# A graph layer with gathered keys and values on one core: the instructions of the last three quads in another order, the last quad cut in three tiles and one, and two normalizations on GpSimd

## The chip, the cores and the metric

The kernel runs on one core of one Trainium2 chip. The metric is device time in microseconds (us), the median of the runs shown; less is better. Beside the runs there is one profiled execution of the kernel, with a trace of its instructions and transfers. Engines are named as in the profile: PE is TensorE's matmul, PEld its weight load, DVE VectorE, ACT ScalarE, POOL GpSimd, SP SyncE, which here only issues transfers. A "q" behind a name (SPq, POOLq) is that engine's sequencer, which issues, waits and branches.

## What is computed

`x` has 6250 nodes of 128 features; there are 206250 edges, sorted by the node `dst` that receives; an edge takes k and v at `src` and q at `dst`, and adds into `dst`.

```python
w = silu(edge_attr_32 @ rad_W1 + rad_b1) @ rad_W2 + rad_b2
w = w + silu(edge_attr_32_n2 @ sph_W1 + sph_b1) @ sph_W2 + sph_b2   # edges x 8 heads x 16
q, k, v = x @ Wq, x @ Wk, x @ Wv                                    # nodes x 8 heads x 16
alpha = (q[dst] * w * k[src]).sum(-1) / sqrt(16) * edge_weight      # edges x 8
out = segment_sum(alpha[..., None] * v[src], dst) / 16
y = x + out
return (y - mean(y)) / sqrt(var(y) + 1e-5)                          # per node
```

## The kernel before

**Tiles.** A tile is 128 edges, a quad 4 tiles (512 edges), a group 4 quads (2048 edges). There are 101 groups (`NG`) and 403 quads; the last group, number 100, has three quads. Within a group the quads are worked on in the order 0, 2, 1, 3 (`order`), so the last three quads of the program are called `a`, `b`, `c` = `order[-3:]`. In SBUF a quad's edges lie on the 128 partitions, 4 tiles of 128 columns each.

**A quad's work.** PE makes the two hidden layers (`first_layers`, L552, tile `ph`), ACT applies silu (`silus`, L584), PE makes q at the edges with a one-hot matrix (`q_at_edges`, L561, tile `pq`) and the second layers with the bias (`weigh`, L599 and L604, tile `pw`). GpSimd gathers k and v of the senders from a table in DRAM (`gathers`, L140, tile `kv`, four transfers a quad, in a ring of 16 buffers that have a semaphore each; `kv_done` holds the semaphore and the count that a quad's reader waits for). DVE then runs, in this order: `multiply` (L618: q times k), `scores` (L626: times w, L628: sum over each head, L632: times the edge's weight) and `messages` (L645: alpha times v). PE sums the messages of a group into four windows of 32 nodes (`sum_quads`, L657, tile `po`), ACT copies them out (`part_sums`, L693), PE places them into the group's 128 nodes and adds what the group before left over (`sum_group`, L698 and L700; its one-hot matrices are made on DVE by `place`, L687 and L688, tile `to`), and ACT copies the total (L702, tile `tot`).

**Rows.** In 60 of the 403 quads the fourth tile's rows are loaded one by one from SP's and ACT's queues (L211, tile `wide`) instead of by GpSimd; quad `b` is one of them, `c` is not.

**Normalization.** `moments` adds x (L715, tile `y`), and takes mean and variance on DVE (L717 `st`, L718 `mv`). For most groups the inverse root is made on DVE (`inverse_roots`), for the last four it is a square root on ACT (`roots`, L723, `sd`) and a reciprocal on DVE (L741, `rs`); ACT then writes the normalized rows (`scaled`, L736) with a `shift` made on DVE (L730), and SP stores them (`write_rows`, L774). Windows of neighbouring groups overlap in `out`, so each store waits until the store before it has landed.

**Order.** Nothing is scheduled by a planner: the program is recorded as written (`tc.manual_schedule`), each engine executes its instructions in that order, and waits are put in from the tiles that are read and written. One iteration of the main loop (from L810) weighs quad i+1, applies silu for i+2, gathers for i+14, multiplies i+1 and makes the messages of i. The loop ends with group 99 (`NG - 2`); what follows, from L881 on, is written out by hand for group 100. There `sum_wide` (L679) adds `a`, `b` and `c` straight into the 128 nodes with wide one-hots (`wide_one_hots`, L665 to L668, tile `hots`, made on DVE in groups 98 and 99; `weigh_wide` puts the edge weights into them on ACT, so that `scores(..., weighted=False)` needs no L632).

**PSUM.** There are two banks each for `ph`, `pq` and `pw`, one for `po` and one that holds `side`. Before, the end uses a `pq` bank for the totals of groups 98 and 99 and a `ph` bank for the sum of group 100.

**After the last store** every engine reaches the branch at L1035 (a general path, not taken with this data) and the closing instructions at L1087.

## Time and profile before

| what | value |
|---|---|
| device time, median of 3 runs | 2671.97 us |
| the three runs | 2673.54, 2659.76, 2671.97 us |
| the profiled execution: its device time | 2669.98 us |
| the profiled execution: its span in the trace | 2668.2 us |
| mean granted TensorE clock in it | 0.814 |
| instructions | 57891 |
| busy: PE, PEld, DVE, ACT, POOL | 2191.4, 1790.8, 1526.5, 651.5, 1472.9 us |

How to read it: the span runs from the first to the last instruction in the trace; the device time has 1.8 us more around it. Rows of the timeline have the start in us, the length in us, the engine, the line, the operation and its operands (result first), and in brackets for how long the engine had been idle and what ended it. Rows of the windows have the stretch, its length, the busy time of PE, PEld, DVE, ACT and POOL with the number of instructions, the granted TensorE clock, the share of the DMA engines' time and GB/s. Rows by line have the engine's sequencer, operation, count, shortest, median and longest duration in ns, and the first and the last start.

### The profile page before, as it was taken

How to read it: one execution, taken by the hardware profiler on the slowest of the kernel's cores; microseconds unless marked ns; L12 is line 12 of the kernel's file. 1: busy time of each engine (PE TensorE's matmuls, PEld its weight loads, DVE VectorE, ACT ScalarE, POOL GpSimd, SP SyncE). 2: the span in 40 equal slices, each digit the busy share in tenths (PEclk: the TensorE clock that was granted, in tenths of full speed). 3: DMA queues.
4: the chain of work that ended last, by engine and by line, in shares of the span. 5: the costliest groups of instructions: out<-in, count | busy, mean ns of one | idle time of the engine just before them, and what ended most of it. 6: DMA issues, size and time to landing. Idle time of an engine off the chain costs nothing.

```text
span 2668.2 us, 57891 instructions
## 1 busy us (share of the span) xinstructions
PE 2191.4 (82%) x15990; PEld 1790.8 (67%) x15990; DVE 1526.5 (57%) x3424; ACT 651.5 (24%) x1360; POOL 1472.9 (55%) x1562
## 2 busy tenths in 40 slices
PE   5688888788888888888887888888788888888888
PEld 3466666676766676666666676676666766667676
DVE  2456555656555555655555655555555555556557
ACT  1122222222222222222222222222222222222223
POOL 4365555555556555555555555555555555555550
PEclk7788878878878887887888878877788787777889
DMA  5433343443334343343434434333333433334331
GB/s 178 137 117 111 114 117 112 118 117 111 116 107 119 109 121 115 112 120 108 121 110 119 119 108 118 112 117 110 115 119 112 116 110 118 116 114 115 116 104 35
DMA packets 154089, 305.48 MB, mean 114 GB/s; under 512 B 40748, under 2 KB 88220, under 8 KB 153756
## 3 DMA queue, kind: packets, MB, share of 16 engines
q0 software_dynamic: 73984, 201.43, 26.8%
q1 hardware_dynamic: 70352, 95.81, 11.0%
q10 hardware_dynamic: 9420, 4.47, 0.7%
q8 instruction: 127, 2.08, 0.3%
q14 instruction: 206, 1.69, 0.2%
HBM read 288.10 MB, written 13.46 MB: 113 GB/s over the span
## 4 chain that ended last, share of the span: by engine, by line
PE 67%; issue 16%; SPq 7%; DVE 6%; another core or an unknown queue 3%; ACTq 0%; DMA 0%; ACT 0%; DVEq 0%
PE pw L604 33%; PE ph L552 10%; PE pq L561 10%; PE po L657 6%; SPq L211 5%; PE pw L599 3%; PE pq L283 2%; PE pq L698 1%; DVE kq L618 1%; PE pk L378 1%; SPq L205 1%; PE pq L700 1%; DVE side L628 1%; PE pq L274 1%
## 5 line engine op out<-in xcount | busy, mean ns | idle before, releaser
L140 POOL DMA_INDIRECT kv<-kv_tab,src_i x1520 | 1440.5, 948 | 1112.2 <-PE pw L604 493.0
L604 PE MATMUL pw<-w,act 128*128 128x128 f32 x6448 | 1091.6, 334 | 70.3 <-issue 69.4
L604 PEld LDWEIGHTS pw<-w,act 128*128 128x128 f32 x6448 | 988.5, 240 | 195.4 <-issue 178.6
L584 ACT ACTIVATE act<-ph,b 128x512 f32<-128x512 f32 x806 | 554.4, 688 | 1899.3 <-PE pw L604 1284.5
L552 PE MATMUL ph<-feats,w 32*128 32x512 f32 x1612 | 677.0, 772 | 149.5 <-issue 141.2
L618 DVE TENSOR_TENSOR kq<-pq,kv 128x512 f32<-128x512 f32 (+1 forms) x403 | 270.7, 672 | 859.6 <-PE pw L604 599.1
L561 PE MATMUL pq<-q,hotT 32*128 32x128 f32 x3224 | 572.9, 328 | 7.1 <-issue 3.6
L561 PEld LDWEIGHTS pq<-q,hotT 32*128 32x128 f32 x3224 | 483.9, 226 | 12.9 <-issue 12.2
L552 PEld LDWEIGHTS ph<-feats,w 32*128 32x128 f32 x1612 | 193.2, 215 | 309.5 <-issue 279.3
L628 DVE TENSOR_REDUCE side<-kq 128x32 f32<-128x512 f32 x403 | 280.1, 695 | 92.2 <-remote 27.4
L645 DVE TENSOR_TENSOR msg<-kv,side 128x512 f32<-128x512 f32 (+1 forms) x404 | 269.4, 667 | 42.8 <-DVE side L632 0.9
L626 DVE TENSOR_TENSOR kq<-pw,kq 128x512 f32<-128x512 f32 x403 | 274.4, 681 | 0.0
L657 PE MATMUL po<-msg,hot 128*32 128x128 f32 x3200 | 191.7, 312 | 33.0 <-issue 32.8
L599 PE MATMUL pw<-brow,onesb 3*128 3x512 bf16 x403 | 182.0, 452 | 0.0
L657 PEld LDWEIGHTS po<-msg,hot 128*32 128x32 f32 x3200 | 84.8, 117 | 90.3 <-issue 63.9
L283 PE MATMUL pq<-wq,xT 128*128 128x128 f32 x200 | 54.7, 362 | 83.6 <-issue 68.0
L698 PE MATMUL pq<-part,to 128*128 128x128 f32 x200 | 53.4, 356 | 68.4 <-issue 34.2
L283 PEld LDWEIGHTS pq<-wq,xT 128*128 128x128 f32 x200 | 35.2, 220 | 109.0 <-issue 88.0
L632 DVE TENSOR_TENSOR side<-side,scale 128x32 f32<-128x32 f32 x400 | 80.0, 200 | 44.9 <-remote 1.7
L698 PEld LDWEIGHTS pq<-part,to 128*128 128x128 f32 x200 | 37.3, 232 | 80.2 <-issue 43.3
L378 PE MATMUL pk<-wkv,xT 128*128 128x256 f32 x162 | 48.5, 442 | 48.3 <-DVE kv L379 39.6
L378 PEld LDWEIGHTS pk<-wkv,xT 128*128 128x128 f32 x162 | 33.3, 221 | 56.9 <-DVE kv L379 38.1
(121 smaller groups left out, 912.9 us busy)
## 6 DMA issues: line engine op xcount, KB each, us to landing
wide<-kv_tab ACTq DMA_DIRECT2D x3960, 1.0 KB
wide<-kv_tab SPq DMA_DIRECT2D x3720, 1.0 KB
feats<-in_edges SPq DMA_DIRECT2D x101, 512.0 KB
kv<-kv_tab,src_i POOLq DMA_INDIRECT x1520
relb<-rel_lin SPq DMA_DIRECT2D x101, 128.0 KB
x<-in_x SPq DMA_DIRECT2D x101, 64.0 KB
out<-y SPq DMA_DIRECT2D x101, 64.0 KB
kv_tab<-kv SPq DMA_DIRECT2D x12, 512.0 KB
```

Of the source, the lines that this page charges most:

```text
L140: return nc.gpsimd.indirect_dma_start(out=o, out_offset=None, in_=table, in_offset=bass.IndirectOffsetOnAxis(ap=index, axis=0))
L283: nc.tensor.matmul(pt[:n, :D], xT_of[g][:, :n], wq, start=True, stop=True)
L552: return nc.tensor.matmul(act_of[q, i], w1[r0:r0 + R, :], feats_of[g][r0:r0 + R, c0:c0 + EQ], start=True, stop=True)
L561: o = nc.tensor.matmul(pq_of[q][:, t, :], hotT_of[g][b, t * P:(t + 1) * P], q_of[g][b, :], start=True, stop=True)
L584: o = nc.scalar.activation(act, act_of[q, i], AF.Silu, bias=b1[:, i:i + 1])
L599: nc.tensor.matmul(pw, onesb, brow.rearrange("p t d -> p (t d)"), start=True, stop=False)
L604: o = nc.tensor.matmul(pw[:, t, :], act_of[q, i][:, t * P:(t + 1) * P], w2[:, i, :], start=False, stop=(t == QT - 1 and i == 1))
L618: o = nc.vector.tensor_tensor(kq_of[q][:, u, :], pq_of[q][:, u, :], kv[:, :, :D], op=OP.mult)
L626: nc.vector.tensor_tensor(m, pw_of[q][:, t, :], m, op=OP.mult)
L628: o = nc.vector.tensor_reduce(alpha, m.rearrange("p t (h e) -> p t h e", e=HD), AX.X, OP.add)
L645: o = nc.vector.tensor_tensor(msg_of[q][:, u, :].rearrange("p t (h e) -> p t h e", e=HD), kv[:, :, D:].rearrange("p t (h e) -> p t h e", e ...
L657: o = nc.tensor.matmul(po_of[g][j * W:(j + 1) * W, :], hot_of[g][:, j * QT + t, :], msg_of[g * NQ + j][:, t, :], start=(t == 0), stop=(t = ...
```

## The change

It does these things, all within groups 97 to 100:

- The fourth tile of the last quad `c` is gathered under a 17th semaphore, and its reader waits for it by itself.
- `multiply`, `scores` and `messages` of `c` are called for tiles 0 to 2 and then for tile 3 instead of for the quad (`messages` had been called for two halves).
- q of `c` is made before the total of group 98; the totals of 98 and 99 use `ph` banks, the sum of group 100 uses the `po` bank. The second layers of `c` come before the total of 99.
- GpSimd adds x for group 98 and 99, as before, and now normalizes them too (subtract the mean, multiply by the inverse root, in one instruction each). ACT's `scaled` and DVE's `shift` for these two are gone; each has a square root and a reciprocal of its own.
- `place` of 98 is made two slots earlier in group 99; `place` of 99 and of 100 and the wide one-hots of `c` are made in group 97 instead of 99.

```diff
-    kv_sems = [tc.alloc_semaphore(f"kv_{n}") for n in range(RING)]
+    kv_sems = [tc.alloc_semaphore(f"kv_{n}") for n in range(RING + 1)]
@@ gathers
+            last = (q, t) == (order[-1], QT - 1)
+            n = RING if last else at
...
-            tc.add_to_no_dep_group(f"kv_{q}", o.ins)
+            tc.add_to_no_dep_group("kv_last" if last else f"kv_{q}", o.ins)
@@ multiply
+            if q == order[-1] and t.stop == QT:
+                waits.append(("kv_last", (kv_sems[RING], kv_count[RING])))
@@
+        def added(g):
+            nc.gpsimd.tensor_tensor(y0(g), tot_of[g], x_of[g], op=OP.add)
@@ main loop
-                if slot == 2 and 1 <= g:
+                if slot == (2 if g < NG - 2 else 0) and 1 <= g:
                     place(g - 1)
...
+                if g == NG - 4 and slot == 0:
+                    place(NG - 2)
+                if g == NG - 4 and slot == 1:
+                    wide_one_hots(order[-1])
+                if g == NG - 4 and slot == 3:
+                    place(NG - 1)
...
                 if g == NG - 2 and slot == 0:
-                    wide_one_hots(order[-1])
                     n = nc.values_load(general, min_val=0, max_val=1)
-                    place(g)
-                    place(NG - 1)
@@ behind the loop
         first_layers(c)
         mark = q_at_edges(b)
-        marks = weigh(b)
-        turned = sum_group(g - 2)
-        for t in range(QT):
-            sum_quads(g - 1, t)
-        silus(c, mark, marks)
+        weigh(b)
+        silus(c, mark)
...
+        def normalized(g, engine, total):
+            i, y = g - (NG - LB), y0(g)
+            engine.tensor_scalar(y, total, y0_of[NG - LB][1][:, i, 0:1], rs[:, i:i + 1],
+                                 op0=OP.subtract, op1=OP.mult)
...
+        roots(g - 3, g - 2)
+        write_rows(len(written))
+        messages(a, scores(a, weighted=False))
+        multiply(b, mark)
+        mark = q_at_edges(c)
+        turned = sum_group(g - 2, "ph")
+        for t in range(QT):
+            sum_quads(g - 1, t)
+        inverses(g - 3, g - 2)
+        shift = shifts(g - 3, g - 2, rs)
+        scaled(g - 3, rs[:, 0:1], shift[:, 0:1], 0)
...
-        mark = q_at_edges(c)
-        turned = sum_group(g - 1)
-        marks = weigh(c)
+        weigh(c)
+        turned = sum_group(g - 1, "ph")
         turned()
-        po_of[g] = pp.tile([P, EQ], F32, name="ph", bufs=2)[:, :D]
+        messages(b, scores(b, weighted=False))
+        po_of[g] = pp.tile([P, D], F32, name="po")
...
-        moments(g - 2, tot_of[g - 2], nc.gpsimd)
-        multiply(c, mark)
-        moments(g - 1, tot_of[g - 1], nc.gpsimd)
-        sd = roots(g - 2, g)
-        normalize(g - 2, g, sd)
-        write_rows(len(written))
-        alpha = scores(c, weighted=False)
-        for h in halves:
-            messages(c, alpha[:, h], h)
-            for t in range(h.start, h.stop):
-                sum_wide(c, t, stop=(t == QT - 1))
-        moments(g, po_of[g], added=True)
+        for i, t in ((g - 2, slice(0, QT - 1)), (g - 1, slice(QT - 1, QT))):
+            added(i)
+            moments(i, None, added=y0(i))
+            roots(i, i + 1)
+            multiply(c, mark if t.start == 0 else None, t)
+            inverses(i, i + 1)
+            normalized(i, nc.gpsimd, y0(i))
+            send(i, nc.sync)
+            messages(c, scores(c, t, weighted=False), t)
+            for i in range(t.start, t.stop):
+                sum_wide(c, i, stop=(i == QT - 1))
+        moments(g, None, added=po_of[g])
...
-        nc.sync.dma_start(out[N - P:, :], y)
+        nc.sync.dma_start(out[N - P:, :], y0(g))
```

**DVE in group 97.** The first place is DVE's order from the one-hots of group 97 (`hot`) to the messages of the loop's second slot. Before:

```order
L294 TENSOR_TENSOR hot<-rel,side 128x512
L618 TENSOR_TENSOR kq<-pq,kv 128x512
L626 TENSOR_TENSOR kq<-pw,kq 128x512
L628 TENSOR_REDUCE side<-kq 128x32
L632 TENSOR_TENSOR side<-side,scale 128x32
L645 TENSOR_TENSOR msg<-kv,side 128x512
L289 TENSOR_TENSOR hotT<-relb,side 128x512
L268 TENSOR_TENSOR pick<-side,off 128x128
L618 TENSOR_TENSOR kq<-pq,kv 128x512
```

The same piece with the change (the lines are numbered anew there: L623 is the old L618, L631 L626, L633 L628, L650 L645):

```order
L692 TENSOR_SCALAR to_42872<-side,rowq 128x128
L693 TENSOR_SCALAR to_42872<-side,rowp 128x128
L623 TENSOR_TENSOR kq<-pq,kv 128x512
L631 TENSOR_TENSOR kq<-pw,kq 128x512
L633 TENSOR_REDUCE side<-kq 128x32
L637 TENSOR_TENSOR side<-side,scale 128x32
L650 TENSOR_TENSOR msg<-kv,side 128x512
L291 TENSOR_TENSOR hotT<-relb,side 128x512
L270 TENSOR_TENSOR pick<-side,off 128x128
L670 CAST d<-dst_i 128x4
L671 TENSOR_SCALAR d<-d,gb 128x4
L673 TENSOR_TENSOR hots<-d,side 128x512
```

Five instructions stand here that stood in group 99, and a sixth (`to` of group 100) follows two slots later.

**DVE at the last quad.** The second place is DVE's order from the mean and variance of group 98 to the end. Before:

```order
L717 BN_STATS st<-y_43818 128x6
L718 BN_AGGR mv<-st 128x2
L618 TENSOR_TENSOR kq<-pq,kv 128x512
L717 BN_STATS st<-y_43818 128x6
L718 BN_AGGR mv<-st 128x2
L741 RECIPROCAL rs<-sd 128x2
L730 SCALAR_TENSOR_TENSOR shift<-mv,rs 128x2
L626 TENSOR_TENSOR kq<-pw,kq 128x512
L628 TENSOR_REDUCE side<-kq 128x32
L645 TENSOR_TENSOR msg<-kv,side 128x256 x2
L717 BN_STATS st<-ph 128x6
```

With the change, from the first `kq` of `c` on:

```order
L623 TENSOR_TENSOR kq<-pq,kv 128x384
L897 RECIPROCAL rs<-sd 128x1
L631 TENSOR_TENSOR kq<-pw,kq 128x384
L633 TENSOR_REDUCE side<-kq 128x24
L650 TENSOR_TENSOR msg<-kv,side 128x384
L728 BN_STATS st<-y_43818 128x6
L729 BN_AGGR mv<-st 128x2
L623 TENSOR_TENSOR kq<-pq,kv 128x128
L897 RECIPROCAL rs<-sd 128x1
L631 TENSOR_TENSOR kq<-pw,kq 128x128
L633 TENSOR_REDUCE side<-kq 128x8
L650 TENSOR_TENSOR msg<-kv,side 128x128
```

The quad's three wide operations are now six, the statistics of group 99 stand between them, and a `shift` is gone.

**GpSimd's end.** The third place is GpSimd's last work before the branch at the end (L1035 before, L1052 with the change). Before:

```order
L140 DMA kv<-kv_tab,src_i 128x256 x1520
L873 TENSOR_LOAD general
L715 TENSOR_TENSOR y_43818<-tot,x 128x128 x2
L1035 COMPARE_AND_BRANCH
L1043 COMPARE_AND_BRANCH
```

With the change:

```order
L140 DMA kv<-kv_tab,src_i 128x256 x1520
L875 TENSOR_LOAD general
L717 TENSOR_TENSOR y_43818<-tot,x 128x128
L901 TENSOR_SCALAR y_43818<-y_43818,mv,rs 128x128
L717 TENSOR_TENSOR y_43818<-tot,x 128x128
L901 TENSOR_SCALAR y_43818<-y_43818,mv,rs 128x128
L1052 COMPARE_AND_BRANCH
L1060 COMPARE_AND_BRANCH
```

Each sum is now followed by its normalization, which reads the reciprocal of its group, and the branch follows the second one.

82 lines of the change are left out of this document (37 added, 45 removed).

## The prediction

> **What bounds the kernel now.** First the chain of waits on the page, by engine: PE holds two thirds of it over the whole span.
>
> ```profile
> PE 67%; issue 16%; SPq 7%; DVE 6%; another core or an unknown queue 3%; ACTq 0%; DMA 0%; ACT 0%; DVEq 0%
> ```
>
> The change begins in group 97, so the view that counts is a table of busy times by stretch, cut where the chain of waits passes from one engine to another (length, then busy us of PE, PEld, DVE, ACT, POOL, then the clock).
>
> ```profile
> 2596.00:2617.30 21.30, 21.04 (x205) 17.60 (x205) 17.56 (x36) 7.21 (x16) 0.00 (x0) 1.00 0.17 52
> 2632.40:2642.30 9.90, 9.21 (x72) 7.73 (x72) 8.62 (x19) 3.35 (x9) 0.00 (x0) 0.66 0.02 4
> 2642.30:2649.84 7.54, 7.54 (x72) 6.47 (x72) 6.84 (x15) 4.25 (x10) 0.00 (x0) 1.00 0.10 27
> 2649.84:2655.20 5.36, 5.30 (x65) 4.47 (x65) 5.19 (x12) 3.79 (x9) 0.65 (x2) 1.00 0.15 43
> 2655.20:2662.20 7.00, 5.05 (x43) 4.67 (x42) 4.97 (x16) 1.47 (x4) 0.27 (x1) 1.00 0.09 23
> 2662.20:2668.20 6.00, 0.00 (x0) 0.00 (x0) 0.00 (x0) 0.00 (x0) 0.00 (x0) 0.63 0.08 19
> ```
>
> In group 97 (first row) PE is full and DVE has 21.30 - 17.56 = 3.74 us to spare. From 2642.3 to 2655.2 both are nearly full, and the chain runs over DVE. At the last quad neither is full: there it is one thing after another. The last 6 us hold no work of a compute engine at all. Before 2596 us nothing is reordered, so 97% of the span can differ only by scatter.
>
> **The work that moves between groups 97 and 99.** Rows of the timeline of DVE:
>
> ```profile
> 2617.34 0.56 DVE L618 TENSOR_TENSOR kq<-pq,kv 128x384 f32<-128x384 f32 x1 [1.33 <-DVEq L615]
> ...
> 2636.04 0.16 DVE L665 CAST d<-dst_i 128x4 f32<-128x4 int32 x1
> ...
> 2637.93 0.68 DVE L618 TENSOR_TENSOR kq<-pq,kv 128x512 f32<-128x512 f32 x1
> ...
> 2642.29 0.69 DVE L618 TENSOR_TENSOR kq<-pq,kv 128x512 f32<-128x512 f32 x1 [0.58 <-PE pq L561]
> ...
> 2645.39 0.34 DVE L687 TENSOR_SCALAR to<-side,rowq 128x128 f32<-128x128 f32 x1
> ...
> 2645.91 0.28 DVE L715 TENSOR_TENSOR y<-tot,x 128x128 f32<-128x128 f32 x1
> ```
>
> The wide one-hots of `c`, two `to` of group 99 and one of group 100 take from 2636.04 to 2637.93, 1.89 us from start to start. They go to group 97. There DVE waits 1.33 us for the rows of a quad that SP loads, at 2617.34; this wait hides as much, and 1.89 - 1.33 = 0.56 us stays, less what DVE's other spare time takes. If PE, the full engine there, isn't held at all it is 0; if the rows came late too, 1.89. I take **+0.3** (nearest to the row with the wait), range 0 to +1.9.
>
> In group 99 the 1.89 us are gone and the two `to` of group 98 come in (2645.39 to 2645.91, 0.52 us). But at 2642.29 DVE waits 0.58 us for PE: what it saves before that it waits longer there. **0**. After 2642.29 DVE is on the path, and the 0.52 us that leave 2645.39 are gained: **-0.52**.
>
> **The end up to the last quad.** Rows of the timeline, all engines:
>
> ```profile
> 2651.90 0.55 DVE L618 TENSOR_TENSOR kq<-pq,kv 128x384 f32<-128x384 f32 x1
> 2652.15 0.29 ACT L723 ACTIVATE sd<-mv,eps 128x1 f32<-128x1 f32 x1
> ...
> 2652.36 0.28 DVE L618 TENSOR_TENSOR kq<-pq,wide 128x128 f32<-128x128 f32 x1
> 2652.56 0.15 DVE L741 RECIPROCAL rs<-sd 128x1 f32<-128x1 f32 x1
> 2652.70 0.46 POOL L715 TENSOR_TENSOR y<-tot,x 128x128 f32<-128x128 f32 x1 [57.13 <-ACT tot L702]
> 2652.75 0.42 DVE L730 SCALAR_TENSOR_TENSOR shift<-mv,rs 128x1 f32<-128x1 f32 x1
> ...
> 2653.09 0.68 DVE L626 TENSOR_TENSOR kq<-pw,kq 128x512 f32<-128x512 f32 x1
> ...
> 2655.01 0.46 POOL L715 TENSOR_TENSOR y<-tot,x 128x128 f32<-128x128 f32 x1 [1.86 <-ACT tot L702]
> 2655.20 0.29 DVE L717 BATCH_NORM_STATS2 st<-y 128x6 f32<-128x128 f32 x1
> ...
> 2655.72 0.69 DVE L618 TENSOR_TENSOR kq<-pq,kv 128x512 f32<-128x512 f32 x1
> ...
> 2656.64 0.18 DVE L718 BATCH_NORM_AGGREGATE mv<-st 128x2 f32<-128x6 f32 x1
> ...
> 2657.19 0.17 DVE L741 RECIPROCAL rs<-sd 128x2 f32<-128x2 f32 x1 [0.36 <-ACT sd L723]
> 2657.39 0.16 DVE L730 SCALAR_TENSOR_TENSOR shift<-mv,rs 128x2 f32<-128x2 f32 x1
> 2657.47 0.68 DVE L626 TENSOR_TENSOR kq<-pw,kq 128x512 f32<-128x512 f32 x1
> ...
> 2658.92 0.75 DVE L645 TENSOR_TENSOR msg<-kv,side 128x256 f32<-128x256 f32 x2
> 2659.39 1.16 PE L679 MATMUL ph<-msg,hots 128*128 128x128 f32 x8 [0.30 <-DVE msg L645]
> 2660.59 0.30 DVE L717 BATCH_NORM_STATS2 st<-ph 128x6 f32<-128x128 f32 x1 [0.92 <-PE ph L679]
> ...
> 2661.72 0.41 DVE L930 TENSOR_SCALAR y<-ph,mv,rs 128x128 f32<-128x128 f32 x1
> ...
> 2662.97 0.34 SPq L931 DMA_DIRECT2D out<-y  x1
> ```
>
> Group 97's reciprocal stands on DVE at 2652.56, right behind ACT's root (2652.15 + 0.29 = 2652.44). ACT's work up to it is not moved. DVE now comes 0.52 us sooner and waits: of the 0.52 only about 0.1 stays, so 0.4 is **given back**. The shift behind it lasted 0.42 us against 0.16 for the same form at 2657.39, while GpSimd's sum ran (2652.70 to 2653.16); from it to the next instruction it is 0.34 against 0.08. With the change GpSimd's first sum comes later, since ACT copies group 98's total behind the rows of group 97. So 0.26 us less, or 0 if the 0.42 has another cause; I take the two rows: **-0.26**. [...]
>
> q of `c`, its second layers and the totals on PE: DVE doesn't wait for PE between 2645 and 2659.39 in these rows, so sooner is worth **0**; what hides them is DVE's own order. The totals now lie behind the second layers, and GpSimd's second sum needs group 99's; DVE asks for it only after 2.8 us of `c` (below). The new semaphore costs 0 too: GpSimd had been idle for 57.13 us at 2652.70, so the last gather left it at 2595.6, 60 us before its reader.
>
> **The last quad.** From 2655.20 to the final statistics at 2660.59 it was 5.39 us. The new order, by rows: statistics of 98 0.52 (2655.20 to 2655.72); `kq` of three tiles 0.46 (2651.90 to 2652.36); reciprocal 0.20 (2657.19 to 2657.39); times w 0.55 + 0.04 and the sum over heads the same (the three-tile length with the gap of a dependent instruction), 1.18; `msg` 0.46; that is 2.82. Statistics of 99 to its reciprocal 0.32 + 0.55 (2656.64 to 2657.19; one-tile `kq` lies inside), reciprocal 0.20, times w and sum 0.32 each (0.28 for one tile, with the gap), `msg` 0.28: 4.81. PE then took 0.92 us from the last `msg` (2658.92 + 0.75 = 2659.67) to 2660.59 with two tiles behind it; one tile less is two of its eight matmuls at 0.145, so 0.63: 5.44. **+0.05**, from -0.3 (if one-tile pieces overlap) to +0.6 (GpSimd late). Two shorter chains have replaced one wait for the root.
>
> **The last stores.** What SP waited for, then the transfers between 2660.6 and 2662.2:
>
> ```profile
> SPq L931 <- DMA out<-y: 2.7, 1, 2.7
> ```
>
> ```profile
> q1 hardware_dynamic: 144, 0.07, 15.1%
> q8 instruction: 1, 0.02, 4.4%
> ```
>
> The final store left at 2662.97 though its data were ready at 2661.72 + 0.41 = 2662.13: it waited for group 99's store, in whose time one packet of instructions was fetched. So group 99's store counts, and GpSimd now feeds it. It starts at 2655.20 + 0.3 - 0.1 - 0.26 + 3.69 + 0.16 = 2659.0; GpSimd's normalization is not in the trace: at least its sum's 0.46, at most 0.9 (twice); DVE's form of it took 0.41 against 0.30 for statistics of the same size, by that ratio 0.63. The store leaves at about 2659.7, near enough to where it must have left before (2662.97 less the wait of 2.7 and the issue before it). **0**, from -0.8 (it lands before the final data) to +0.3.
>
> **GpSimd's closing work.** Sequencer rows of the branch (L1035), then of the closing (L1087); counts, shortest/median/longest ns, first and last start:
>
> ```profile
> L1035 POOLq COMPARE_BRANCH  x1: 53/53/53, 2655.0 to 2655.0; - x1
> L1035 POOLq INC_SWDGE_SEM  x1: 976/976/976, 2657.9 to 2657.9; - x1
> ```
>
> ```profile
> L1087 POOLq EVENT_SEMAPHORE  x4: 17/17/17, 2667.2 to 2668.1; - x4
> L1087 POOLq DRAIN  x3: 40/135/6357, 2658.9 to 2667.9; - x3
> L1087 SPq DRAIN  x3: 7/7/136, 2667.0 to 2667.5; - x3
> ```
>
> Behind its last sum (2655.01) GpSimd branches, and then drains for 6.36 us from 2658.9 to 2665.3; all engines meet at 2667.2, when SP has seen the final store land. GpSimd was 1.9 us early. Its last operation now starts at 2659.0, 4.0 us later. If branch and drain follow it by the same 10.3 us, the drain ends at 2669.3: **+2.1** beyond 2667.2. If the drain ends by something else it is 0; more than 4.0 - 1.9 it isn't. No other engine shows an event at 2665.3, so I take +2.1.
>
> **The sum.** +0.3 + 0 - 0.1 - 0.26 + 0.05 + 0 = 0.0 for the path over the stores; GpSimd's closing outlasts it by 2.1. Span 2668.2 + 2.1 = 2670.3, device time 2669.98 + 2.1 = 2672.1 against this execution. The three runs shown have 2659.76 to 2673.54 and the profiled one 2669.98; their mean is 2668.8, and 2668.8 + 2.1 gives **2671 us**, 1 below the median of 2671.97. A difference under 0.5% (13.4 us) can't be told from none on this kernel.
>
> **Rivals.**
> - *GpSimd's drain does not follow its last operation* (0.33). For it: a drain of 40 and one of 135 ns stand beside it, so 6.36 us is no fixed price. Against: nothing else ends with it. The sum is then 0.0, or -0.8 if group 99's store misses the fetch: 2668 to 2669.
> - *PE falls out of full clock in group 97* (0.06). The 1.89 us of DVE work delay the `kq` that frees PE's banks; PE idles long enough for the clock to fall as in the row of 2632.4 (0.66). At 0.66 the 21.04 us of PE become 31.9, +10.9; at half, +21. Half way, +16: 2668.8 + 2.1 + 16 = 2687, **slower**. It decides once DVE needs more than its 3.74 us there; 1.89 is half of that, hence the low chance. [...]
> - *The end is shorter than the rows say* (0.11): GpSimd's work hides, the pieces of `c` overlap, no fetch hits a store: -0.3 - 0.8 - 0.3 = -1.4, 2667 us.
> - *The change doesn't do what it says*: the order shows that it does.
>
> **How the numbers follow.** The forecast, 2671, has 0.50. All cases but the clock lie within 2667 and 2671, so the range is made by scatter: four executions spread over 13.8 us, and both medians share it. 2660 to 2680 leaves about 2 in 10 outside, the clock among them. Faster by over 0.5% is below 2658.6: a median that falls on the lowest run shown or below, 0.10. Slower is above 2685.3: the clock, 0.06, and scatter, 0.03: 0.09. Within: 0.81.
>
> **What would show it.** Right: GpSimd's drain begins at about 2663 and ends last, behind SP's; reciprocal of group 97 waits about 0.4 us for ACT; final data within 0.5 us of 2662.1. Wrong: the drain still ends near 2665 or is short; the wait for rows at 2617 stays 1.3 us; DVE waits for GpSimd at group 99's statistics; PE's clock below 1 in group 97; or any difference before group 97 larger than that behind it, which would be scatter.

## The result, and the profile after

| | before | after |
|---|---|---|
| device time, median (lowest to highest), 14 runs each | 2666.05 us (2659.76 to 2673.54) | 2668.39 us (2659.79 to 2676.54) |
| after / before, 95% interval | | 1.0007 (0.9995 to 1.0020) |
| profiled execution: device time, span | 2669.98, 2668.2 us | 2676.54, 2674.8 us |

No difference can be told in the time: the interval allows anything from 1.3 us less to 5.3 us more. In the experiments below, the kernel before takes 2657 to 2680 us on some chips and 1985.5 and 1990.4 us on two others; in three profiles taken there (no GpSimd, root first, spread roots without the moves) PE waits 0.2 to 4.5 us in all, instead of some 340 to 360, for what the profile calls "issue", and why is open.

The rows tell more than the time. Two executions differ by several microseconds before the first reordered instruction stands (here by 4.98 us, up to VectorE's one-hots of group 97 at 2598.42 and at 2603.40), so everything below is counted from that instruction, or from the statistics of group 98. The busy times by stretch (length, then busy us of PE, PEld, DVE, ACT, POOL, then the clock), cut at VectorE's one-hots of group 97, those of group 99, the second multiply of group 99, the statistics of group 98 and those of group 100. Before:

```profile
2598.42:2635.44 37.02, 32.62 (x305) 26.91 (x305) 31.85 (x77) 14.63 (x32) 0.00 (x0) 0.97 0.16 47
2635.44:2642.29 6.85, 6.85 (x52) 6.02 (x52) 5.88 (x14) 3.34 (x8) 0.00 (x0) 0.68 0.01 3
2642.29:2655.20 12.91, 12.85 (x135) 10.95 (x135) 12.04 (x26) 8.06 (x17) 0.65 (x2) 1.00 0.12 34
2655.20:2660.59 5.39, 5.05 (x43) 4.67 (x42) 3.92 (x13) 1.18 (x3) 0.27 (x1) 1.00 0.05 15
```

After, at the same places:

```profile
2603.40:2640.19 36.79, 32.73 (x313) 27.40 (x311) 33.41 (x83) 14.61 (x32) 0.00 (x0) 0.99 0.15 47
2640.19:2645.54 5.35, 5.35 (x46) 4.51 (x42) 4.58 (x10) 3.34 (x8) 0.00 (x0) 0.77 0.02 3
2645.54:2658.12 12.58, 12.58 (x133) 10.72 (x133) 11.36 (x24) 7.76 (x16) 0.46 (x1) 1.00 0.09 24
2658.12:2664.78 6.66, 5.54 (x45) 4.97 (x44) 4.34 (x15) 0.75 (x3) 2.02 (x3) 1.00 0.11 31
```

The lengths differ by -0.23, -1.50, -0.33 and +1.27 us. What is left of the span behind the last cut was 2668.2 - 2660.6 = 7.6 and is 2674.8 - 2664.8 = 10.0 us: +2.4. Together +1.6 from group 97 on, where 2.1 was forecast. But the parts are not those of the forecast: the start of group 99 (second row) is 1.5 us shorter, at a mean clock of 0.77 instead of 0.68, and the last quad and the end are 3.7 us longer, not 2.1. One sign that the prediction had named against itself came true: the 4.98 us ahead of the first reordered instruction are more than the 1.6 behind it, so the difference of these two executions in time is mostly scatter.

The last quad and the stores, from the timeline of all engines after:

```profile
2655.73 0.16 DVE L897 RECIPROCAL rs<-sd 128x1 f32<-128x1 f32 x1 [0.34 <-ACT sd L893]
2655.92 0.16 DVE L734 SCALAR_TENSOR_TENSOR shift<-mv,rs 128x1 f32<-128x1 f32 x1
...
2658.44 0.18 DVE L729 BATCH_NORM_AGGREGATE mv<-st 128x2 f32<-128x6 f32 x1
...
2660.10 0.28 ACT L707 ACTIVATE tot<-ph 128x128 f32<-128x128 f32 x1 [2.44 <-PE ph L705]
2660.27 0.28 ACT L893 ACTIVATE sd<-mv,eps 128x1 f32<-128x1 f32 x1
2660.59 0.17 DVE L897 RECIPROCAL rs<-sd 128x1 f32<-128x1 f32 x1 [1.40 <-ACT sd L893]
2660.95 0.79 POOL L901 TENSOR_SCALAR y<-y,mv,rs 128x128 f32<-128x128 f32 x1 [3.62 <-DVE rs L897]
...
2663.54 0.79 POOL L901 TENSOR_SCALAR y<-y,mv,rs 128x128 f32<-128x128 f32 x1 [1.37 <-DVE rs L897]
...
2665.86 0.41 DVE L901 TENSOR_SCALAR y<-po,mv,rs 128x128 f32<-128x128 f32 x1
...
2667.88 0.34 SPq L947 DMA_DIRECT2D out<-y  x1
```

The input of group 98's root was ready at 2658.44 + 0.18 = 2658.62, but ACT started it only at 2660.27: ahead of it in ACT's order stands the copy of group 99's total, which waited 2.44 us for PE. DVE's reciprocal waited 1.40 us in its turn. At the end, `y` was ready at 2665.86 + 0.41 = 2666.27, and its store left at 2667.88, 1.61 us later (0.84 before).

Sequencer rows of the branch, then of the closing (counts; shortest/median/longest ns; first and last start):

```profile
L1052 POOLq COMPARE_BRANCH  x1: 53/53/53, 2663.5 to 2663.5; - x1
```

```profile
L1104 POOLq DRAIN  x3: 45/142/6362, 2667.4 to 2674.5; - x3
L1104 SPq DRAIN  x3: 7/7/136, 2672.0 to 2674.0; - x3
```

GpSimd reaches the branch at 2663.5, with its last normalization, and its long drain runs from 2667.4 to 2673.74. SP had seen the final store land at 2672.0. Before, SP came last (2667.0, drain ended 2665.3); now the drain does, by 1.7 us.

### The profile page after: what moved, and what is told of

Read it like the earlier page. It is cut to its first block, busy times and chain, and to the rows that moved or that the text cites. A ratio compares the mean times of both kernels' runs of the same rounds, so it can differ in the third digit from the quotient of the medians.

```text
span 2674.8 us, 57896 instructions
## 1 busy us (share of the span) xinstructions
PE 2180.6 (82%) x15990; PEld 1783.9 (67%) x15990; DVE 1527.1 (57%) x3427; ACT 649.9 (24%) x1359; POOL 1469.9 (55%) x1564
## 3 DMA queue, kind: packets, MB, share of 16 engines
q1 hardware_dynamic: 70352, 95.81, 10.8%
## 4 chain that ended last, share of the span: by engine, by line
PE 73%; issue 15%; DVE 6%; another core or an unknown queue 4%; SPq 1%; ACTq 1%; ACT 0%; DMA 0%; DVEq 0%
PE pw L606 36%; PE ph L554 11%; PE pq L563 11%; PE po L662 6%; PE pw L601 3%; PE pq L285 2%; PE pq L703 2%; DVE kq L623 1%; PE pq L705 1%; PE pk L380 1%; DVE side L633 1%; PE pq L276 1%; SPq L213 1%; DVE kq L631 1%
## 5 line engine op out<-in xcount | busy, mean ns | idle before, releaser
L554 PE MATMUL ph<-feats,w 32*128 32x512 f32 x1612 | 670.2, 766 | 150.0 <-issue 136.5
L623 DVE TENSOR_TENSOR kq<-pq,kv 128x512 f32<-128x512 f32 (+1 forms) x404 | 270.7, 670 | 853.9 <-PE pw L606 596.9
L563 PE MATMUL pq<-q,hotT 32*128 32x128 f32 x3224 | 565.8, 325 | 6.2 <-issue 3.6
L563 PEld LDWEIGHTS pq<-q,hotT 32*128 32x128 f32 x3224 | 478.0, 223 | 11.3 <-issue 10.9
L633 DVE TENSOR_REDUCE side<-kq 128x32 f32<-128x512 f32 x404 | 280.2, 694 | 102.3 <-PE pw L606 33.8
L650 DVE TENSOR_TENSOR msg<-kv,side 128x512 f32<-128x512 f32 (+1 forms) x404 | 269.4, 667 | 42.9 <-PE pq L563 1.0
L631 DVE TENSOR_TENSOR kq<-pw,kq 128x512 f32<-128x512 f32 x404 | 274.5, 679 | 0.0
L285 PE MATMUL pq<-wq,xT 128*128 128x128 f32 x200 | 54.8, 362 | 101.1 <-issue 77.2
L381 DVE COPY kv<-pk 128x512 f32<-128x512 f32 (+1 forms) x41 | 27.2, 679 | 74.1 <-remote 56.5
```

Source lines behind the costliest of these rows:

```text
L554: return nc.tensor.matmul(act_of[q, i], w1[r0:r0 + R, :], feats_of[g][r0:r0 + R, c0:c0 + EQ], start=True, stop=True)
L563: o = nc.tensor.matmul(pq_of[q][:, t, :], hotT_of[g][b, t * P:(t + 1) * P], q_of[g][b, :], start=True, stop=True)
L623: o = nc.vector.tensor_tensor(kq_of[q][:, u, :], pq_of[q][:, u, :], kv[:, :, :D], op=OP.mult)
L631: nc.vector.tensor_tensor(m, pw_of[q][:, t, :], m, op=OP.mult)
L633: o = nc.vector.tensor_reduce(alpha, m.rearrange("p t (h e) -> p t h e", e=HD), AX.X, OP.add)
L650: o = nc.vector.tensor_tensor(msg_of[q][:, u, :].rearrange("p t (h e) -> p t h e", e=HD), kv[:, :, D:].rearrange("p t (h e) -> p t h e", e ...
```

## The experiments

Their profiles are compared in us from the statistics of group 98 (`st98`), since what stands ahead differs by scatter: to the statistics of group 100, to the final data (`y` ready), to SP's first closing drain (the final store has landed), to the end of GpSimd's long drain, and to the end of the span. The column at the right is from the start of GpSimd's last operation to the end of its long drain.

| kernel | st100 | `y` | SP | GpSimd's drain | end | last operation to drain's end |
|---|---|---|---|---|---|---|
| before | 5.39 | 6.93 | 11.8 | 10.1 | 13.0 | 10.3 |
| after | 6.66 | 8.15 | 13.9 | 15.6 | 16.6 | 10.2 |
| no GpSimd work at the end | 7.43 | 8.92 | 12.0 | -15.6 | 13.5 | (a gather) |
| before, one late sum on GpSimd | 5.39 | 6.94 | 12.1 | 17.4 | 18.4 | 10.3 |
| root first | 5.59 | 7.07 | 12.4 | 14.8 | 15.8 | 10.5 |
| moves undone | 6.59 | 8.08 | 14.4 | 15.6 | 16.6 | 10.2 |
| root first, quad whole | 7.42 | 8.90 | 12.0 | 14.5 | 15.5 | 10.4 |
| total first | 6.75 | 8.23 | 14.5 | 15.7 | 16.7 | 10.2 |
| best end (two profiles) | 6.11, 6.12 | 7.60, 7.60 | 10.8, 10.6 | 9.1, 9.1 | 11.9, 11.8 | 10.3, 10.3 |

**GpSimd's closing.** Two runs ask whether the drain follows GpSimd's last operation. In the first, nothing is left to it at the end:

```diff
-            nc.gpsimd.tensor_tensor(y0(g), tot_of[g], x_of[g], op=OP.add)
+            nc.vector.tensor_tensor(y0(g), tot_of[g], x_of[g], op=OP.add)
...
-            normalized(i, nc.gpsimd, y0(i))
+            normalized(i, nc.vector, y0(i))
```

> The changed kernel, with the two sums and the two normalizations of groups 98 and 99 on VectorE instead of GpSimd; GpSimd's last operation is then the last gather's issue, some 60 us before the end. Times are counted from VectorE's one-hots of group 97, where the changed kernel had the end of GpSimd's drain at 70.3, the end of SyncE's wait at 68.6 and the end of the span at 71.4. Theory (the closing follows GpSimd's last operation by 10.2 us): the long drain ends some 50 us before the end and sets nothing; the span ends about 1.1 us behind SyncE's last wait. VectorE has 0.28 + 0.28 + 0.41 + 0.41 = 1.4 us more to do, of which up to 1.4 lie in its wait for the root of group 98, so SyncE's wait ends at 68.6 to 70 and the span at 69.7 to 71. Rival (the drain ends with something else, the other engines or the last store): it still lasts 6.36 us and ends within 4 us of the span's end.

Rows of GpSimd's timeline (its last gather), then of the closing:

```profile
1945.22 0.95 POOL L140 DMA_INDIRECT kv<-kv_tab,src_i  x1 [0.30 <-issue]
```

```profile
L1104 POOLq DRAIN  x3: 40/142/25605, 1933.6 to 1987.6; - x3
L1104 SPq DRAIN  x3: 7/7/137, 1986.7 to 1987.1; - x3
```

The drain began while gathers were still to be worked off, lasted 25.6 us and ended at 1959.2, 29 us ahead of the span's end (1988.2), which follows SP by 1.5 us. So it doesn't end with the other engines, and neither its end nor its length is fixed; it was not some 50 us early as expected: it ended 13 us behind the last gather. Counted from the one-hots of group 97, SP's wait ended at 67.1 us and the span at 68.6, sooner than the 68.6 to 70 and 69.7 to 71 expected; the final store, whose data came 0.8 us later than in the changed kernel, left 0.03 us behind them. The second run gives the kernel before one late operation:

```diff
         nc.sync.dma_start(out[N - P:, :], y)
+        late = gp.tile([P, D], F32, name="late")
+        nc.gpsimd.tensor_tensor(late, y, x_of[g], op=OP.add)
```

> The kernel before, with one sum of 128x128 on GpSimd behind the final normalization (it reads y of group 100 and is read by nobody). In the kernel before, counted from VectorE's one-hots of group 97, the final data were ready at 63.7, GpSimd's drain ended at 66.9, SyncE's wait at 68.6 and the span at 69.8. Theory (the closing follows GpSimd's last operation by 10.2 us): the sum starts at about 63.8, the drain ends at about 74.1 and the span at about 75.1, 5.3 us later than before, while the final store leaves when it did. Rival (the drain has an end of its own or is shorter when it comes late): the drain ends before 70 and the span is within 1 us of before.

Its timeline, then its closing:

```profile
1979.42 0.45 POOL L933 TENSOR_TENSOR late<-y,x 128x128 f32<-128x128 f32 x1 [6.50 <-DVE y L930]
1980.64 0.34 SPq L931 DMA_DIRECT2D out<-y  x1
```

```profile
L1089 POOLq DRAIN  x3: 40/135/6357, 1983.4 to 1990.5; - x3
L1089 SPq DRAIN  x3: 7/7/136, 1984.5 to 1990.0; - x3
```

One sum of 0.45 us that nobody reads makes the kernel end 5.4 us later (18.4 against 13.0): the drain runs 1983.4 to 1989.8, while the final store had landed at 1984.5. In all nine profiles of the table with a sum or a normalization as GpSimd's last operation the drain ends 10.2 to 10.5 us behind that operation's start. The theory holds.

Most experiments were timed once, so that their times decide nothing and their rows are read instead. Where the kernel before took 1985.52 us, the two runs above took 1990.03 and 1992.55, the one with the root first 1996.27 and the one with the moves undone 1991.77 us. Where it took 2666.23 (13 runs, 2657.49 to 2671.22), the one with the quad whole took 2672.72, the one with the total first 2688.43 (its one-hots of group 97 came at 2614.6, 16 us later than before, so most of that lies ahead of the change), and the first one with the best end 2676.66 us. The rows of the end don't depend on this: the kernel before at 2669.98 us and the one with a late sum at 1992.55 have 5.39 us to st100 and 6.93 and 6.94 to `y`.

**The root behind the copy.**

```diff
         turned = sum_group(g - 1, "ph")
-        turned()
         messages(b, scores(b, weighted=False))
+        added(g - 2)
+        moments(g - 2, None, added=y0(g - 2))
+        roots(g - 2, g - 1)
+        turned()
...
-            added(i)
-            moments(i, None, added=y0(i))
-            roots(i, i + 1)
+            if i > g - 2:
+                added(i)
+                moments(i, None, added=y0(i))
+                roots(i, i + 1)
```

> The changed kernel, with ScalarE's root of group 98 ahead of its copy of the total of group 99; all else as it was. Theory (ScalarE works in order: the root, whose input was ready, stood behind a copy that waited 2.44 us for TensorE's sum, which now lies behind the second layers): VectorE's wait of 1.40 us at group 98's reciprocal falls to 0.1 or less, the statistics of 98 to those of 100 take 5.2 to 5.5 us instead of 6.66, and GpSimd's last operation and its drain's end come about 1.3 us sooner (counted from the one-hots of group 97: 69.0 instead of 70.3). Rival (the split itself, or GpSimd's total, holds the last quad): the wait moves to the statistics of group 99 or to the last matmuls, and the stretch stays above 6.3 us.

The timeline of that run:

```profile
1979.20 0.29 ACT L893 ACTIVATE sd<-mv,eps 128x1 f32<-128x1 f32 x1 [1.00 <-DVE mv L729]
...
1979.66 0.15 DVE L897 RECIPROCAL rs<-sd 128x1 f32<-128x1 f32 x1
...
1980.14 0.56 DVE L631 TENSOR_TENSOR kq<-pw,kq 128x384 f32<-128x384 f32 x1 [0.33 <-PE pw L606]
...
1985.32 0.41 DVE L901 TENSOR_SCALAR y<-po,mv,rs 128x128 f32<-128x128 f32 x1
1987.39 0.34 SPq L951 DMA_DIRECT2D out<-y  x1
```

The reciprocal no longer waits, and st100 comes 1.07 us sooner (5.59), though 0.1 later than expected: next in line, 0.33 us late, are PE's second layers of `c`. GpSimd's last operation comes 1.1 us sooner too (4.3 instead of 5.4 behind st98), and its drain ends 0.8 us sooner, where 1.3 was expected. The theory holds, its size a little smaller. The final store leaves 1.0 us sooner, with its data, but still waits 1.66 us (from 1985.73 to 1987.39) for group 99's store, which comes from GpSimd as in the changed kernel.

The same wait can be taken away on PE instead:

```diff
+        turned = sum_group(g - 1, "ph")
         weigh(c)
-        turned = sum_group(g - 1, "ph")
         turned()
```

> The changed kernel with TensorE's total of group 99 ahead of the second layers of the last quad, as before the change; all else as changed, so that ScalarE's copy of it still stands ahead of the root of 98. Theory 1 (only the late total made the root wait): VectorE's wait of 1.40 us at group 98's reciprocal is gone, and the statistics of 98 to those of 100 take 5.5 us instead of 6.66. Theory 2 (TensorE is the next to be late: the total needs ScalarE's copy of the rows of 99, which ends 0.5 us behind the point where the second layers began, and then the 2.05 us of second layers follow): the wait goes to the weighting of the last quad, on TensorE's second layers, with about 0.9 us more than the 0.33 us of the run with the root first, and the stretch is 6.2 to 6.5 us.

```profile
2672.56 0.56 DVE L631 TENSOR_TENSOR kq<-pw,kq 128x384 f32<-128x384 f32 x1 [1.50 <-PE pw L606]
```

This row of its timeline is theory 2: the wait has passed to the second layers, 1.50 us, and st100 is at 6.75, a little above the 6.2 to 6.5 expected. So it isn't enough to have the total early: in the changed order DVE waits for whichever of the two PE does second. Of the two remedies only ACT's order shortened the stretch.

**The split of the last quad.** On the run with the root first:

```diff
-            multiply(c, mark if t.start == 0 else None, t)
+            if i == g - 2:
+                multiply(c, mark)
             inverses(i, i + 1)
             normalized(i, nc.gpsimd, y0(i))
             send(i, nc.sync)
-            messages(c, scores(c, t, weighted=False), t)
-            for i in range(t.start, t.stop):
-                sum_wide(c, i, stop=(i == QT - 1))
+        messages(c, scores(c, weighted=False))
+        for i in range(QT):
+            sum_wide(c, i, stop=(i == QT - 1))
```

> The run with the root first, and the last quad whole again, in the order of the kernel before: its multiply between the statistics of 98 and of 99, everything else of it behind both normalizations. From the statistics of group 98 to those of 100 the kernel before took 5.39 us, the changed one 6.66, the run with the root first 5.59. Theory 1 (the split costs 0.2 us of its own, by its shorter pieces): 5.4 us. Theory 2 (the split buys the room that TensorE's later total needs: GpSimd's sum of group 99 is ready 2.8 us behind the statistics of 98 and VectorE now asks for it after 1.2): VectorE waits about 1.6 us for GpSimd at the statistics of 99 and the stretch is about 7.0 us.

```profile
2658.31 0.29 DVE L728 BATCH_NORM_STATS2 st<-y 128x6 f32<-128x128 f32 x1 [1.45 <-POOL y L717]
```

Theory 2: DVE waits 1.45 us for GpSimd's sum at group 99's statistics, and st100 is at 7.42. The 0.4 us above the expected 7.0 are PE's: the messages aren't cut in halves here, as they were before, so that eight matmuls stand behind them instead of four, and PE took 1.49 us from the last message to st100 where it had taken 0.92. The split doesn't shorten DVE's work; it fills the time until GpSimd's sum of group 99 is there. The later total is only part of that wait: its copy ended at 2657.21, but GpSimd was normalizing group 98 until 2657.84 and began the sum then. So the split, the later totals and GpSimd's normalization belong together.

**The moves, and the clock.**

```diff
-                if slot == (2 if g < NG - 2 else 0) and 1 <= g:
+                if slot == 2 and 1 <= g:
...
-                if g == NG - 4 and slot == 0:
-                    place(NG - 2)
-                if g == NG - 4 and slot == 1:
-                    wide_one_hots(order[-1])
-                if g == NG - 4 and slot == 3:
-                    place(NG - 1)
...
                 if g == NG - 2 and slot == 0:
+                    wide_one_hots(order[-1])
+                    place(g)
+                    place(NG - 1)
```

> The changed kernel with the wide one-hots of the last quad, the two one-hots of group 99 and the one of group 100 back at the start of group 99, and those of group 98 back in its third step; the end as changed. Counted from VectorE's one-hots of group 97, the second multiply of group 99 began at 43.9 before and at 42.1 after. Theory of the prediction (TensorE paces the start of group 99, so the moved 1.89 us were worth nothing there, and the difference is scatter of one execution): 42.1 within 0.4, as in the other runs with the changed end. Rival (the one-hots stood on VectorE ahead of the multiply that frees TensorE's bank, so TensorE waited for them in its turn): 43.9 within 0.4, while the runs that keep the moves show 42.1. From there to the statistics of group 98 both expect 12.6 + 0.5 - 0.3 = 12.8 us, with no wait at group 97's reciprocal.

The second multiply of group 99 came 43.3 us behind the one-hots of group 97, as the rival says; but in the run with the root first, which keeps the moves, it came at 43.6, and in the one without GpSimd, which keeps them too, at 42.3. Neither theory fits; what differs is PE's clock. (From there to st98 it took 12.65 us without a wait at the reciprocal, close to the 12.8 that both expected.) Windows of 10 us that begin 33 us behind the one-hots of group 97, first the kernel before:

```profile
2631.42:2641.42 10.00, 8.33 (x64) 7.13 (x67) 9.14 (x23) 3.34 (x8) 0.00 (x0) 0.66 0.02 3
```

Then the changed kernel, the run with the root first, and the kernel before with a late sum:

```profile
2636.40:2646.40 10.00, 8.56 (x79) 7.38 (x80) 8.78 (x20) 4.20 (x11) 0.00 (x0) 0.83 0.02 3
```

```profile
1955.48:1965.48 10.00, 8.56 (x68) 7.36 (x70) 8.03 (x18) 3.34 (x8) 0.00 (x0) 0.66 0.09 13
```

```profile
1951.10:1961.10 10.00, 8.67 (x96) 7.13 (x96) 9.24 (x20) 5.14 (x12) 0.00 (x0) 1.00 0.09 15
```

A mean of 0.66 is 6.8 us of the ten at half clock, 0.83 is 3.4 us, 1.00 none. By windows of 0.5 us it is, at this place, 6.82 or 6.83, 3.41, or 0 us, and nothing between. What stands ahead is one wait of PE for DVE's multiply in group 98. Its rows after, and in the kernel with a late sum:

```profile
2637.84 0.49 PE L703 MATMUL pq<-part,to 128*128 128x128 f32 x2 [3.20 <-DVE kq L623]
```

```profile
1951.21 0.49 PE L698 MATMUL pq<-part,to 128*128 128x128 f32 x2 [2.26 <-DVE kq L618]
```

From the one-hots of group 99 to its second multiply:

| | idle of PE in group 98 | at half clock | length |
|---|---|---|---|
| before | 3.19 | 6.82 | 6.85 |
| moves undone | 3.20 | 6.83 | 6.93 |
| root first (moves kept) | 2.99 | 6.83 | 6.81 |
| best end, two profiles (moves kept) | 3.19, 3.20 | 6.83, 6.83 | 6.65, 6.42 |
| after; no GpSimd; total first (moves kept) | 3.20; 3.20; 2.83 | 3.41 | 5.35 each |
| before with a late sum (no moves) | 2.26 | 0 | 6.19 |

At the long half clock the moves are worth 0.0 to 0.5 us. With the moves the stretch takes 5.35 us at 3.41 us of half clock and 6.42 to 6.81 at 6.83, three profiles each: of the 1.5 us that group 99 gained in the profile after, 1.1 to 1.5 are the shorter half clock, which the same moves lack in three of six profiles.

To see the moves without the clock, the wait itself was taken away. It comes from a chain of twelve short operations of DVE (the inverse roots of four groups, 2.4 us in one piece, every fourth group). On the best end below they were spread:

```diff
+                for _ in range(min(2 if g < NG - 2 else 3, len(steps))):
+                    steps.pop(0)()
...
-READY_LAG = 2
+READY_LAG = 8
```

where each operation of `inverse_roots` is appended to `steps` instead of being issued at once.

> The run before it, and every batch's inverse roots (twelve short operations of VectorE in a chain, 2.4 us in one piece every fourth group) spread over the six following steps, two to a step (over four for the last batch); the normalization that needs them is put off by six steps. In the runs so far on this chip TensorE waited for VectorE's multiply behind such a chain some 20 times, 61 us in all, and after several of these waits the granted clock was 0.5 for 3.4 or 6.8 us. Theory (these waits and the clock behind them are what the start of group 99 showed, and they cost every fourth group): the waits fall below 20 us in all, the mean clock rises above 0.95, TensorE is busy at full clock in groups 98 and 99, and the time is 40 to 100 us below the kernel before. Rival (the gathers or TensorE's work elsewhere pace the loop, and the waits move to them): the time is within 0.5% of the kernel before.

> The run with the spread inverse roots again. Where TensorE idles mostly for what the profile calls issue (some 350 us in all, as in the first run of it, at about 2666 us), theory and rival both expect no difference to the kernel before, within 0.3%. Where TensorE idles mostly behind VectorE's multiply (the executions at about 1990 us), the theory (each chain costs its wait and, in part, the clock) expects 40 to 100 us less than the kernel before; the rival (the waits move elsewhere) expects less than 10 us.

Both times it ran at about 2666 us: 2667.72 us, ratio 1.0007 (0.9992 to 1.0022), and 2666.45 us, 0.9992 (0.9974 to 1.0010). In groups 98 and 99 it did what was meant: no idle time of PE as long as 1 us, clock 1.00 in the same 10 us, and the one-hots of group 99 come 17.8 us behind those of 98 instead of 19.9. But part of the last spread chain then stands behind the second multiply of group 99, and from there to st98 it takes 13.9 us instead of 12.6. Over the kernel it gained nothing, and the theory's other signs failed: PE's waits for DVE's multiply were 33 and 51 us in all in the two profiles (29 before; below 20 expected), the mean clock 0.814 and 0.797 (above 0.95 expected). PE's largest waits here are for "issue". The waits of PE in the second run of it (total us, times, longest):

```profile
PE ph L554 <- issue: 128.5, 102, 2.4
PE pw L606 <- issue: 78.5, 114, 1.3
PE pq L285 <- issue: 73.0, 49, 3.3
PE pk L380 <- DVE kv L381: 45.1, 8, 11.9
PE pq L285 <- DVE kq L623: 34.9, 26, 5.5
```

So the rival holds at this level; the second run, at the same level, couldn't decide between the two. Then the moves were undone on top of it, by the same edit as above:

> The run with the spread inverse roots, and the moves undone as in the run of that name. With the roots spread TensorE has no wait of 2 us or more in group 98 and no half clock at the start of group 99, so that the moves can be read without it. From the one-hots of group 99 to its second multiply it was 5.27 us with the moves, in both executions; with half clock it was 6.4 to 6.8 us with the moves and 6.9 without. Theory (the price of the moved one-hots is hidden only because TensorE is slow there; at full clock VectorE paces the start of group 99): 6.7 us or more, that is 1.4 us dearer than with the moves. Rival (TensorE paces it at full clock too): 5.3 to 5.6 us. In group 97 both expect 15.6 to 15.7 us from one-hots to one-hots, where the moves make it 16.8.

The one-hots of group 99 and its second multiply, first with the moves (the second run), then without:

```profile
2643.13 0.68 DVE L296 TENSOR_TENSOR hot<-rel,side 128x512 f32<-128x512 f32 x1
2648.40 0.68 DVE L623 TENSOR_TENSOR kq<-pq,kv 128x512 f32<-128x512 f32 x1
```

```profile
1951.03 0.68 DVE L296 TENSOR_TENSOR hot<-rel,side 128x512 f32<-128x512 f32 x1
1957.62 0.68 DVE L623 TENSOR_TENSOR kq<-pq,kv 128x512 f32<-128x512 f32 x1
```

It took 6.59 us (6.7 or more expected) against 5.27 in both profiles with the moves, at full clock in all three: the moves are worth 1.3 us there. But they are paid for ahead of it. From one-hots to one-hots group 97 took 16.05 us (15.6 to 15.7 expected), where the moves make it 16.8 or more, and over the whole piece from the one-hots of group 97 to st98 it is 54.8 us without the moves and 53.9 and 54.8 with them: between nothing and 0.9 us is left. This one ran where the kernel before took 1990.36 us; it took 1985.36, one run each, and the 40 to 100 us that the theory of the spread expected there aren't to be seen either.

**The best end.** On the run with the root first:

```diff
-            nc.gpsimd.tensor_tensor(y0(g), tot_of[g], x_of[g], op=OP.add)
+            engine = nc.gpsimd if g == NG - 3 else nc.vector
+            engine.tensor_tensor(y0(g), tot_of[g], x_of[g], op=OP.add)
...
-            normalized(i, nc.gpsimd, y0(i))
+            k = i - (NG - LB)
+            s = shifts(i, i + 1, rs[:, k:k + 1])
+            nc.scalar.activation(y0(i), y0(i), AF.Identity, scale=rs[:, k:k + 1], bias=s[:, 0:1])
             send(i, nc.sync)
```

> The run with the root first, with nothing on GpSimd behind its sum of group 98: the sum of group 99 on VectorE, and both normalizations on ScalarE (a shift of 0.16 us on VectorE each). Theory (the closing follows GpSimd's last operation, and VectorE's path sets the rest): the drain ends about 1 us ahead of SyncE's last wait and no longer ends last; from the statistics of 98 to those of 100 about 6.0 us, and to the end of the span 12.9 to 13.5 us (before 13.0, changed 16.6). Rival (the stores, not GpSimd, set it): the stretch to the end of the span stays above 15 us.

> The run with the best end again, timed in five rounds. Its one profile had 11.9 us from the statistics of group 98 to the end of the span, against 13.0 before and 16.6 changed; up to there the moved one-hots cost or gain under 1 us. Theory: 1 us below the kernel before and 4 to 5 us below the changed one in the rows of the end again, which is 0.04% and 0.17% of the time: the ratio to the kernel before is 0.998 to 1.001 and can't be told from 1. Rival (the end's gain is scatter of one execution): 13 us or more from the statistics of 98 to the end.

Its timeline in the second profile, and its closing:

```profile
2658.06 0.49 ACT L945 ACTIVATE y<-y,shift,rs 128x128 f32<-128x128 f32 x1 [0.43 <-DVE shift L735]
...
2660.53 0.41 DVE L902 TENSOR_SCALAR y<-po,mv,rs 128x128 f32<-128x128 f32 x1
2660.97 0.34 SPq L954 DMA_DIRECT2D out<-y  x1
```

```profile
L1111 POOLq DRAIN  x3: 40/142/6357, 2656.0 to 2664.9; - x3
L1111 SPq DRAIN  x3: 7/7/136, 2664.0 to 2664.4; - x3
```

The final store leaves 0.03 us behind its data, the drain ends 1.6 us ahead of SP, and from st98 to the end it is 11.8 us: 1.2 less than before, 4.8 less than the changed kernel, and a microsecond better than the 12.9 expected. In time it is 2667.87 us, ratio to before 0.9998 (0.9982 to 1.0013), as expected: an end that is better by rows, and too small to be measured.

## Why the prediction was right, point by point

The forecast (2671 us, within 0.5%) held, and so did what it forecast to end last. The number itself says little: 2671 is 2.6 us above the measured 2668.39 mostly because it started from a mean of 2668.8 where 14 runs have 2666.05, and neither 2.1 us nor 0 lies outside the interval. Three of its terms were wrong: two cost more than forecast, and one, put at nothing, gained.

- *"Work moved into group 97: +0.3"* (0 to +1.9). From the one-hots of group 97 to those of group 99 the profiles without the moves have 37.0, 35.5 and 36.4 us (before, late sum, moves undone), six with the moves 36.6 to 37.4 (the run with the quad whole, 41.0, is left out, since VectorE waited 3.33 us for rows there): +0.6 on the means of 36.3 and 36.9. The wait for rows of 1.33 us at 2617 is gone in the profile after, as forecast; but it is no sure sign, since the kernel before with a late sum has none either, and the run with the quad whole has 3.33 us of it with the moves. Right; PE's clock was 1.00 from the one-hots of group 97 to those of group 98 in the profile after (2603.40 to 2620.25), so the slower rival has no case.
- *Group 99's start, "what it saves before that it waits longer there. 0"*. Right at the long half clock (0.0 to 0.5 us), and wrong as a statement on PE: its pace there was the clock's, and at full clock the same moves are worth 1.3 us there (and cost 0.8 to 1.7 us in groups 97 and 98 in the same profiles). The wait of 0.58 us was read as PE being full, when the row of the clock beside it, 0.66, said why PE was slow; how long such a dip lasts was not asked.
- *The `to` that leave (-0.52), 0.4 "given back" at group 97's root, the shift (-0.26)*: together -0.36. The stretch went from 12.91 to 12.58, -0.33; the reciprocal waits 0.34 us for ACT, and the shift takes 0.16. The kernel before with a late sum shows the overlap alone: its order is the same up to there, but GpSimd's sum ran 0.9 us ahead of the shift, which took 0.16 us, and the stretch 12.65. So the 0.26 us went with the overlap (0.42 us with GpSimd's sum beside the shift, 0.16 without), and the kernel before doesn't pay them in every execution; why the overlap costs them is not shown. Beside GpSimd's normalization, in the profile after, DVE's multiplication by w and its sum over the heads took 0.56 us each for three tiles (from 2660.68 and 2661.27), against 0.55 and 0.56 in the run without GpSimd.
- *The totals behind the second layers: "0 ... DVE asks for it only after 2.8 us of `c`"*. **This step failed.** It followed the total only to GpSimd's sum of group 99, and forgot what stands behind the copy on ACT: the root of group 98. In order, the root waited for a total it doesn't need; DVE waited 1.40 us for it. Mending ACT's order brings 1.07 us back. By this the prediction's sign "final data within 0.5 us of 2662.1" failed too: counted from st98 they came 1.22 us later, at 2666.27.
- *The last quad, "+0.05"*: +1.27, of which 1.07 is that wait. With the root first it is 5.59 against 5.39, inside the -0.3 to +0.6 given.
- *The last stores, "0"* (-0.8 to +0.3): group 99's store was put at 4.5 us behind st98 and left at 6.2; the final store waited 1.61 us for it instead of 0.84, so +0.8, out of the range. GpSimd's normalization took 0.79 us, not 0.63, and came late by the root.
- *GpSimd's closing, "+2.1"*: the mechanism is shown by two runs, and the 10.3 us of the forecast are 10.2 to 10.5 in all of them. GpSimd's last operation starts 5.4 us behind st98, not the 3.8 forecast, by the late root and its longer normalizations. But SP was itself later by 2.1 us (1.2 of the final data, 0.8 of the store), so the drain outlasts it by less than forecast: the span now ends 2.8 us behind SP's drain instead of 1.2, +1.6.

The sum came near (2.1 forecast, 1.6 in the rows) by luck: the 1.3 us of the last quad and the 0.8 of the store were paid for by the 1.5 us at the start of group 99, of which at least 1.1 are a shorter half clock that the change doesn't own. At equal clock the rows make the changed kernel some 2.7 to 3.1 us slower than before, 0.1% of its time, within what the interval of the ratio allows.

## What to carry to other kernels

An instruction that is made to wait later holds back everything behind it on its engine (here ACT's copy waited 2.44 us for PE, and DVE 1.40 us for the root behind the copy): when a producer is put off, list what stands behind each of its consumers, not only who reads the value. An engine that is idle at the end isn't free if it has to be closed down: here the kernel ended 11.2 to 11.5 us behind the start of GpSimd's last operation wherever GpSimd's drain was last, even when that was a sum of 0.45 us. And an end whose gain is a thousandth of the time is judged by rows counted from a common instruction, in several profiles, since one piece of half clock more or less (1.1 to 1.5 us at the start of group 99) is about as large as the whole change (1.6 us in the rows).

## What was not expected of the hardware

- By the trace's own record of the granted clock, half clock comes, before and after, in whole multiples of 3.413 us (157 and 155 pieces; a last piece cut off by the end of the span apart), and within each of these two profiles all its pieces begin on one raster of that period, to 5 ns. Most are 3.41 to 10.24 us long, the longest 37.5. At the start of group 99 they are 3.41 or 6.83 us long. Idle times of PE of the same length were followed by different pieces there. In the profile after 3.20 us lay in two periods as 1.20 and 2.00, with 3.41 us of half clock behind them; with the moves undone 3.20 us lay as 0.61 and 2.58, with 6.83 behind them; with the late sum 2.26 us had none behind them. In the nine profiles with half clock in groups 97 to 99, by windows of 0.5 us up to the statistics of group 98, a period with up to 1.4 us of idle time was followed by none, one with 1.8 to 2.0 by one period of half clock, and one with 2.3 to 3.2 by two. Over the whole span, before and after, periods with as little as 0.32 and 0.35 us of idle time were followed by half clock too, and some with as much as 1.86 and 1.91 by none, so these are no limits for other places, and what decides it is not shown.
- GpSimd's long drain is 6.36 us behind an arithmetic operation and was 25.6 us where gathers were still being worked off; it ended 13 us behind the last of them.
- GpSimd normalized 128x128 in 0.79 us where DVE took 0.35 with both operands in SBUF, and summed it in 0.46 where DVE took 0.28.
